# Score operands in two float32r parts, scores over the row groups of the array, merged mask and maximum, and bias rows in the matmul, in a one-core decoder layer

## The chip, the core and the metric

The kernel runs on one core of a Trainium2 chip. A core has a matrix engine (PE, with its weight loads listed apart as PEld), a vector engine (DVE), a scalar engine (ACT), GpSimd (POOL), and a queue engine (SP) that issues DMA transfers. On-chip memory is SBUF; matmuls write to PSUM, which has eight banks of 128 x 512 float32. Every engine runs its own instruction stream in order, and semaphores connect the streams. The metric is device time in microseconds from one launch; the profile's span reaches from the first to the last instruction.

## What is computed

One decoder layer over 32 batches of 128 tokens, width 512, in float32: self-attention of 16 heads with rotary embedding and a causal mask, cross-attention over the token axis (8 heads of 16 tokens, 512 x 512 scores for each head), and a feed-forward part with ternary weights and activations in int8 steps. A layer norm follows each.

```python
x = _layernorm(x + _L0_attn_ref(x, Wq, Wk, Wv, Wo))          # softmax(mask(q k^T / sqrt(32))) v
x = _layernorm(x + _L0_xattn_ref(x, ctx, ctx, gamma))        # q, k, v: [batch, 8 heads, 16, 512]
#   qk = einsum('bhdq,bhdl->bhql', qh, kh) / 4;  ret = einsum('bhql,bhdl->bhdq', softmax(qk), vh)
x = _layernorm(x + _L0_ffn_ref(x, w1, b1, ln_g, ln_b, w2, b2))
#   h = silu(bitlinear158(x, w1, b1)); h = gelu(h); h = layer_norm(h, ln_g, ln_b)
#   return bitlinear158(h, w2, b2)    # act_quant(rms_norm(x)) @ weight_quant(w).T + b
```

## The kernel before

**Two phases.** Phase one does the self-attention of all 32 batches and prepares the operands of the cross-attention in DRAM. Phase two does the cross-attention and the feed-forward part, again batch by batch. Work of several batches overlaps inside each phase.

**The order.** The class `Plan` fixes the order of every engine's instructions before the program runs. Each operation has a kind ("PE.sc"), a cost in microseconds, inputs, outputs and a priority; of the operations that could come next, the one is taken that can start first by these costs, with ties by priority plus an offset per kind (`OFF1`, `OFF2`). The order is then fixed with dependencies, so an engine waits for the next instruction in its list even if a later one could go. All transfers are issued from SP, in order. Transfers that prefetch have a release time: 17.8 us a batch in phase one and 30 us a batch in phase two.

**Phase one, per batch.** `project` (L322) multiplies with float32 accuracy in three one-pass float32r products of high and low parts, twelve matmuls of 128 x 512 for q, k, v and the output projection each. `rope` rotates, transposes (L402) turn q and k, and `head` (L412) does four heads at a time: h counts the 32-row groups of the transposed q and k, and c the four chunks. For each h there are four float32 matmuls into one bank (L419), the mask is added on DVE (L422), the maximum is taken (L425), ACT computes four exponentials with their sums (L430), and the weights are divided by the sums (L435) and transposed (L442). `stage_o` weighs the values (L461, four column groups in turn), projects and normalizes. `split3` (L326) writes q and the context as three bfloat16 parts, on DVE, POOL and ACT, and stores six copies of parts for each (L339). PSUM is divided by use: three banks for projections, three for transposes, one for scores, one for the weighed sums.

**Phase two, per batch.** For each group of four heads, `b1_` computes all scores once to find the largest of every query: 16 matmuls of 96 rows in bfloat16 (L653; six products of parts for each of 16 tokens), each followed by a maximum on DVE (L657). `shift` splits the negated maxima into three bfloat16 parts on POOL (L676 to L680), transposes them (L685), copies them on DVE (L687) and stores them as three further rows of the query operand (L691). `b2_` then computes the scores turned, with 99 rows (L746), takes exponentials on ACT (L749), and sums with the context (L756). `final` divides, adds and normalizes through small transfers: F (L767), den (L828), num (L829), rd (L835), rden (L836), and x1 (L830). `up_` quantizes the rows (`scales`, `steps`), multiplies with the ternary weights (L933) and lets DVE scale and add the bias b1 (L936) into z. `gelu_` (L942) is one ACT operation of silu and gelu over 2048 columns, so its table loads stand together. `down_` normalizes z (L963; parts of 512 columns, the first on ACT at L780, the others on POOL), scales it by g and b (L980), quantizes it in two halves on ACT (L897) and DVE (L899) with a conversion (L902), multiplies (L1017), and adds to x2 + b2, which POOL made (L920).

## Time and profile before

Three runs took 1843.21, 1843.22 and 1847.17 us. The profiled execution is one more.

| what | value |
|---|---|
| median of the runs | 1843.22 us |
| span of the profiled execution | 1837.6 us |
| mean granted PE clock | 0.960 of full speed |
| last score of phase one (L419) | 663.2 us |
| first score of phase two (L653) | 683.5 us |
| last maximum of phase two (L657) | 1713.1 us |
| DMA | 275.75 MB, mean 150 GB/s |

The profile's page splits the span into 40 slices and gives the busy share of each in tenths. PE's weight loads are at 7 of ten in the first 14 slices and at 2 to 3 after them, which shows the two phases. Its groups by line give, for each kind of instruction, busy time, the mean of one, and the idle time in front of it with the releaser. The durations of one engine can overlap, above all PE's, so two counts are used in this document: the duration of a group, and the distance between the starts of neighbours in the timeline.

### The profile page before, as it was taken

How to read it: one execution, taken by the hardware profiler on the slowest of the kernel's cores; microseconds unless marked ns; L12 is line 12 of the kernel's file. 1: busy time of each engine (PE TensorE's matmuls, PEld its weight loads, DVE VectorE, ACT ScalarE, POOL GpSimd, SP SyncE). 2: the span in 40 equal slices, each digit the busy share in tenths (PEclk: the TensorE clock that was granted, in tenths of full speed). 3: DMA queues.
4: the chain of work that ended last, by engine and by line, in shares of the span. 5: the costliest groups of instructions: out<-in, count | busy, mean ns of one | idle time of the engine just before them, and what ended most of it. 6: DMA issues, size and time to landing. Idle time of an engine off the chain costs nothing.

```text
span 1837.6 us, 29788 instructions
## 1 busy us (share of the span) xinstructions
PE 1694.8 (92%) x9540; PEld 848.8 (46%) x9540; DVE 1630.8 (89%) x2811; ACT 1337.6 (73%) x2811; POOL 1256.5 (68%) x1903
## 2 busy tenths in 40 slices
PE   6999999999999989999999999999999998889864
PEld 5877777777777762232323333333333322222221
DVE  7789998889988868898989999999999989999885
ACT  3556545664545544789999989999999979878862
POOL 4466666656656550467798989899889986775562
PEclk9999999999999987998999999999999999989976
DMA  6466656665654564543545455454544543533422
GB/s 197 136 212 210 193 191 205 210 212 187 203 175 161 174 212 171 149 116 106 148 122 159 110 134 147 126 149 117 151 137 128 154 118 110 147 106 102 97 61 57
DMA packets 237733, 275.75 MB, mean 150 GB/s; under 512 B 112124, under 2 KB 161276, under 8 KB 237192
## 3 DMA queue, kind: packets, MB, share of 16 engines
q1 hardware_dynamic: 237576, 273.85, 50.2%
q8 instruction: 75, 1.23, 0.3%
q14 instruction: 82, 0.67, 0.1%
HBM read 150.82 MB, written 101.20 MB: 137 GB/s over the span
## 4 chain that ended last, share of the span: by engine, by line
PE 47%; DVE 23%; DMA 9%; ACT 7%; POOL 6%; issue 4%; SPq 1%; DVEq 0%; POOLq 0%; ACTq 0%
PE mm L322 14%; DVE mt L657 7%; PE sT L746 7%; PE acc L756 7%; PE mx L653 6%; PE sc L419 5%; ACT ex L749 3%; PE m L933 3%; PE m L1017 2%; DMA qd<-sp 2%; PE tr L442 2%; DMA q2T<-q 1%; DVE z L936 1%; DVE pr L422 1%; DMA qp<-qd 1%
## 5 line engine op out<-in xcount | busy, mean ns | idle before, releaser
L657 DVE TENSOR_REDUCE mt<-mx 128x1 f32<-128x512 f32 x1024 | 642.4, 678 | 42.7 <-PE mx L653 41.5
L749 ACT ACTIVATE ex<-sT 128x512 f32<-128x512 f32 x1024 | 535.6, 618 | 90.7 <-PE sT L746 71.8
L653 PE MATMUL mx<-kp,qp 96*128 96x512 bf16 x1024 | 342.3, 393 | 34.4 <-DVE mt L657 28.4
L746 PE MATMUL sT<-qp,kp 99*128 99x512 bf16 x1024 | 322.9, 388 | 10.8 <-ACT ex L749 6.3
L756 PE MATMUL acc<-ex,cT 128*32 128x512 f32 x2048 | 275.7, 613 | 0.7 <-DMA cT<-cd 0.7
L430 ACT ACTIVATE pr<-pr,nm 128x128 f32<-128x128 f32 x512 | 199.5, 392 | 103.9 <-DVE nm L425 87.2
L653 PEld LDWEIGHTS <-qp 96*128 96x128 bf16 x1024 | 96.5, 99 | 221.9 <-issue 120.9
L746 PEld LDWEIGHTS <-kp 99*128 99x128 bf16 x1024 | 88.3, 98 | 222.5 <-issue 146.5
L445 ACT COPY prT<-tr 128x512 f32<-128x512 f32 x96 | 52.9, 587 | 149.2 <-PE tr L442 149.0
L419 PE MATMUL sc<-qkT,qkT 32*128 32x128 f32 x1024 | 147.8, 283 | 11.6 <-DVE pr L422 11.1
L933 PE MATMUL m<-w1q,q1T 128*128 128x512 fp8e4 x512 | 137.4, 392 | 22.0 <-DVE z L936 12.4
L419 PEld LDWEIGHTS sc<-qkT,qkT 32*128 32x128 f32 x1024 | 123.4, 186 | 52.2 <-DVE pr L422 22.1
L980 POOL TENSOR_TENSOR z<-z,g_b 128x512 f32<-128x512 f32 x108 | 139.5, 1302 | 4.9 <-ACT z L780 4.3
L980 POOL TENSOR_TENSOR z<-z,bb_b 128x512 f32<-128x512 f32 x108 | 139.8, 1301 | 1.4
L435 POOL TENSOR_TENSOR pr<-pr,rd 128x512 f32<-128x512 f32 x96 | 106.4, 1108 | 45.9 <-DVE rd L433 31.8
L386 POOL TENSOR_TENSOR ra<-ra,rb 128x256 f32<-128x256 f32 x64 | 47.3, 738 | 117.4 <-DVE rb L381 117.1
L1017 PE MATMUL m<-w2q,q2T 128*128 128x512 fp8e4 x432 | 112.3, 388 | 3.8 <-DMA q2T<-q 2.8
L422 DVE TENSOR_TENSOR pr<-sc,cmask 128x512 f32<-128x512 f32 x128 | 86.8, 678 | 18.3 <-PE sc L419 10.1
L1017 PEld LDWEIGHTS <-q2T 128*128 128x128 f16 x512 | 52.3, 104 | 105.0 <-DMA q2T<-q 29.1
L936 DVE SCALAR_TENSOR_TENSOR z<-m,dq,b_b 128x512 f32<-128x512 f32 x128 | 94.9, 741 | 6.0 <-PE m L933 5.4
L430 ACT ACTIVATION_READ_ACCUMULATOR pr<-pr,nm 128x1 f32 x512 | 96.5, 189 | 0.0
L756 PEld LDWEIGHTS acc<-ex,cT 128*32 128x32 f32 x2048 | 41.2, 108 | 119.5 <-issue 112.8
(159 smaller groups left out, 3475.3 us busy)
## 6 DMA issues: line engine op xcount, KB each, us to landing
kd<-sp SPq DMA_DIRECT2D x192, 128.0 KB
qd<-sp SPq DMA_DIRECT2D x192, 128.0 KB
kp<-kd SPq DMA_DIRECT2D x64, 384.0 KB
qp<-qd SPq DMA_DIRECT2D x64, 384.0 KB
cd<-v SPq DMA_DIRECT2D x32, 512.0 KB
cT<-cd SPq DMA_DIRECT2D x32, 512.0 KB
F<-f SPq DMA_DIRECT2D x64, 256.0 KB
xt<-in_xT SPq DMA_DIRECT2D x32, 256.0 KB
```

Of the source, the lines that this page charges most:

```text
L322: nc.tensor.matmul(pq.t, parts[a].t[:, c, :], w[t][:, c, sl], start=k == 0, stop=k == 11)
L419: nc.tensor.matmul(sc.t[:, c * P:(c + 1) * P], qT.t[r, c, :], kT.t[r, c, :], start=True, stop=True)
L430: nc.scalar.activation(pr.t[:, c, :], pr.t[:, c, :], AF.Exp, bias=nm.t[:, c:c + 1], accum_out=den.t[:, c:c + 1])
L653: nc.tensor.matmul(sc.t[:, j, :], q.t[0:NPR, h, (qc + j) * P:(qc + j + 1) * P], k.t[0:NPR, h, :], start=True, stop=True)
L657: pl.op("DVE.mx", 0.064 + 0.534 * W, lambda: nc.vector.tensor_reduce(mt.t[:, i:i + W], sc.t, AX.X, ALU.max), (sc,), (mt,), p, join=True)
L746: nc.tensor.matmul(sc.t[:, i, :], k.t[:, h, lc * P:(lc + 1) * P], q.t[:, h, :], start=True, stop=True)
L749: pl.op("ACT.ex", 0.052 + 0.426 * SW, lambda: nc.scalar.activation(ex.t[:, j:j + SW, :], sc.t, AF.Exp, scale=1.0 / XD ** 0.5), (sc,), (ex, ...
L756: nc.tensor.matmul(acc.t[32 * h:32 * h + 32, :], v.t[:, XH * lc + 4 * g + h, :], exs[h // 2].t[:, h % 2, :], start=lc == 0, stop=lc == NC - 1)
L933: nc.tensor.matmul(flat(pz)[:, i * 512:(i + 1) * 512], q1T.t[:, c, :], w1q[:, c, (n + i) * 512:(n + i + 1) * 512], start=c == 0, stop=c == ...
L936: pl.op("DVE.z", 0.13 + 0.535 * W, lambda: nc.vector.scalar_tensor_tensor(z.t[:, sl], flat(pz), dq1.t, b1_b[:, sl], ALU.mult, ALU.add), (p ...
L980: pl.op(e + kind, 0.148 + 0.0021 * w if e == "Pool" else 0.05 + 0.00105 * w, lambda: en(e).tensor_tensor(t(), t(), other[:, sl], op), src, ...
L1017: nc.tensor.matmul(flat(py)[:, 0:D], q2T.t[:, c, :], w2q[:, c, :], start=c == 0, stop=c == NI - 1)
```

## The change

**Phase one.** The scores of all four groups of heads become one operation of 16 matmuls, chunk by chunk over the four row groups, into four banks. Adding the mask and taking the maximum become one call for each chunk, of the negated masked score and its minimum; the exponential then has scale -1. The split makes two float32r parts instead of three bfloat16 ones, and two transfers of 256 KB each. All eight banks of PSUM are shared by all uses, in both phases. The biases b1 and b2 are split in two parts and stored as three rows each.

**Phase two.** A score operand has 48 rows (three products of parts for 16 tokens) and one row for the shift. Two heads lie in one tile, at partitions 0 and 64. The maxima are transposed in float32, without the split. An operand is fetched in four transfers instead of one. The bias enters as a last matmul of three rows, scaled by the inverse of the row's scale (`inverse`), so that silu on ACT reads PSUM directly with the row's scale. Silu is four operations of 512 columns, and a window in the planner keeps exponentials of other batches out between a batch's first silu and its gelu. The normalization of z is all on POOL, and the second quantization is one addition on POOL and one subtraction on DVE. The sums with the context are cut into two halves of 256 columns, but for the first chunk. The planner prices the second of two neighbouring score matmuls of opposite halves at 0.06 us, and a table load at 1.28. Offsets, buffers and release times (15 and 29 us a batch) are set anew, and comments are gone.

```diff
-NPR = 6 * XD
-NROW = NPR + 3
+NPR = 3 * XD
+NROW = NPR + 1
+HALF = 64
...
+            if o.engine == "PE":
+                if o.half is not None and self.half == 1 - o.half and t < self.free.get("PE", 0.0) + 0.02:
+                    o.end, self.half = t + self.BESIDE, None
+                else:
+                    self.half = o.half
+            if o.tab:
+                if self.table not in (None, o.tab):
+                    o.end += self.LOAD
+                self.table = o.tab
+                self.window = None if o.closes else o.win
...
+    def fetch(t, d, g, keys):
+        rows = t.bitcast(F32).rearrange("(p r) j c -> p r j c", p=2)
+        src = d[:, :, 4 * g:4 * g + 4, :].rearrange("s t (p j) c -> p (s t) j c", p=2)
+        for p in range(2):
+            if keys:
+                nc.sync.dma_start(rows[p, 0:XD], src[p, 0:XD])
+                nc.sync.dma_start(rows[p, XD:NPR], src[p])
+            else:
+                nc.sync.dma_start(rows[p, 0:2 * XD], src[p])
+                nc.sync.dma_start(rows[p, 2 * XD:NPR], src[p, 0:XD])
...
-                ("sp", C1["sp"], (P, 3, D), BF16), ("spr", C1["spr"], (P, D), F32), ("cx", 2, (P, D), F32),
+                ("sp", C1["sp"], (P, 2, D), F32R), ("cx", 2, (P, D), F32),
...
-            for s, k in enumerate(parts):
-                dma(kind, lambda s=s, k=k: nc.sync.dma_start(dst[s].rearrange("t h c -> h t c"), sp.t[:, k, :]), 131,
+            pl.op(f"{e1}.{kind}l", 0.6 if e1 == "DVE" else 1.225, lambda: en(e1).tensor_tensor(
+                sp.t[:, 1, :], v.t, sp.t[:, 0, :].bitcast(F32), ALU.subtract), (v, sp), (sp,), prio)
+            for s in range(2):
+                dma(kind, lambda s=s: nc.sync.dma_start(dst[s].rearrange("t h c -> h t c"), sp.t[:, s, :].bitcast(F32)), 262,
                     (sp,), (), prio)
...
+            scs = [pl.buf("sc") for _ in range(4)]
+            def scores():
+                for c in range(NC):
+                    for h in range(4):
+                        r = slice(32 * h, 32 * h + 32)
+                        nc.tensor.matmul(scs[h].t[:, c * P:(c + 1) * P], qT.t[r, c, :], kT.t[r, c, :],
+                                         start=True, stop=True)
+            pl.op("PE.sc", C1['scc'], scores, (qT, kT), scs, at + 0.2)
...
-                pl.op("DVE.mask", 0.6, lambda: nc.vector.tensor_tensor(
-                    pr.t, sc.t.rearrange("p (a b) -> p a b", b=S), cmask.unsqueeze(1).to_broadcast([P, 4, S]), ALU.add),
-                    (sc,), (pr,), p)
-                pl.op("DVE.nm", 0.6, lambda: nc.vector.tensor_reduce(nm.t, pr.t, AX.X, ALU.max, negate=True),
-                      (pr,), (nm,), p)
+                def top():
+                    for c in range(NC):
+                        nc.vector.tensor_tensor_reduce(pr.t[:, c, :], sc.t[:, c * P:(c + 1) * P], cmask, -1.0, 3e38,
+                                                       ALU.add, ALU.min, nm.t[:, c:c + 1])
+                pl.op("DVE.mask", 0.8, top, (sc,), (pr, nm), p)
...
+            def half(h):
+                sc, i, r = pl.buf("mx"), 8 * h + 4 * j + qc, slice(HALF * h, HALF * h + NPR)
+                pl.op("PE.mx", 0.23, lambda: nc.tensor.matmul(sc.t, q.t[r, j, qc * P:(qc + 1) * P], k.t[r, j, :],
+                                                             start=True, stop=True), (q, k), (sc,), p, half=h)
...
+            m = 1 if lc == 0 else 2
+            for i in range(m):
+                pl.op("PE.pv", 0.96 / m, lambda cols=slice(D // m * i, D // m * (i + 1)), last=lc == NC - 1 and i == m - 1: weigh(cols, last), exs + [v], (acc,), p)
...
+        def inverse():
+            e = en(e2)
+            r = ut.t.rearrange("p (g r) -> p g r", r=32)
+            if e2 == "DVE":
+                nc.vector.reciprocal(u.t, dq.t)
+            else:
+                nc.gpsimd.tensor_tensor(u.t, dq.t, none, ALU.pow)
+            e.tensor_scalar(r[:, :, 0:3:2].bitcast(F32R), u.t.unsqueeze(2).to_broadcast([P, 4, 2]), 1.0, None, ALU.mult)
+            e.tensor_tensor(r[:, :, 1], u.t.to_broadcast([P, 4]), r[:, :, 0], ALU.subtract)
...
-            pl.op("DVE.z", 0.13 + 0.535 * W, lambda: nc.vector.scalar_tensor_tensor(z.t[:, sl], flat(pz), dq1.t, b1_b[:, sl],
-                                                                         ALU.mult, ALU.add), (pz, dq1, consts[0]), (z,), at, join=True)
+                if last:
+                    nc.tensor.matmul(pz.t, uT.t[32 * n:32 * n + 3, :], rows1[32 * n:32 * n + 3, :], start=False, stop=True)
+            pl.op("ACT.silu", 0.478, lambda: nc.scalar.activation(z.t[:, sl], pz.t, AF.Silu, scale=dq1.t),
+                  (pz, dq1), (z,), at, join=True, tab="silu", win=win)
...
+                if n == 7:
+                    nc.tensor.matmul(py.t, uT.t[0:3, :], rows2, start=False, stop=True)
```

In the settings, `q2m='ad'` becomes `q2m='mp'`, `zm='APPP'` becomes `zm='PPPP'`, and the buffers `x2` 2 to 4, `z` 3 to 4 and `q1T` 2 to 4. In the changed file the scores of phase one are L469, the merged mask L481, the two scores of phase two L716 and L779, the sums L788, and silu L983.

## The prediction

> **What bounds the kernel now.** The change touches both phases, so I first split the span with the view of busy time by stretch and then price each phase in its steady part.

> ```profile
> span 1837.6 us, 29788 instructions
> PE 1694.8 (92%) x9540; PEld 848.8 (46%) x9540; DVE 1630.8 (89%) x2811; ACT 1337.6 (73%) x2811; POOL 1256.5 (68%) x1903
> ...
> 350.00:400.00 50.00, 49.44 (x325) 39.79 (x324) 39.81 (x78) 31.21 (x111) 30.91 (x38) 1.00 0.69 232
> ...
> 950.00:1250.00 300.00, 287.23 (x1488) 93.18 (x1485) 284.52 (x467) 279.61 (x417) 267.88 (x451) 0.99 0.49 133
> ```

> Columns: stretch, its length, busy time of PE, PE's weight loads, DVE, ACT, POOL, granted clock, DMA share, GB/s. Phase one is one engine's: PE never stops (49 of 50 us); DVE averages 88% from 100 to 600 us. Phase two has four loaded engines: DVE 95%, ACT 93%, POOL 89%, and a PE figure that overlapping records inflate. The DMA queues are half empty and the clock is full: neither bounds.

> Periods: the stores of x1 stand at 96.1 and 420.9 us with 16 batches between, so **20.3 us a batch** in phase one. The silu table loads stand at 918.5 and 1182.0 with 8 between: **32.9 us a batch** in phase two. Per batch of phase two that makes DVE 31.2 us, ACT 30.7, POOL 29.4 (284.52, 279.61, 267.88 over 9.1 batches).

> PE has to be counted start to start, from its timeline:

> ```profile
> 333.53 1.10 PE L322 MATMUL mm<-woh,ol 128*128 128x512 f32 x4
> 334.47 0.60 PE L402 MATMUL tr<-ident,ra 128*128 128x128 f32 x4
> 334.82 1.18 PE L322 MATMUL mm<-wol,oh 128*128 128x512 f32 x4
> ...
> 337.77 1.15 PE L419 MATMUL sc<-qkT,qkT 32*128 32x128 f32 x8
> 338.85 1.08 PE L461 MATMUL po<-prT,v 128*32 128x128 f32 x32
> 339.86 1.20 PE L322 MATMUL mm<-wvh,xh 128*128 128x512 f32 x4
> 340.99 1.15 PE L419 MATMUL sc<-qkT,qkT 32*128 32x128 f32 x8
> 342.08 1.20 PE L322 MATMUL mm<-wvh,xl 128*128 128x512 f32 x4
> ...
> 1107.65 0.81 PE L746 MATMUL sT<-qp,kp 99*128 99x512 bf16 x3
> 1108.39 1.06 PE L756 MATMUL acc<-ex,cT 128*32 128x512 f32 x8
> 1109.39 0.82 PE L746 MATMUL sT<-qp,kp 99*128 99x512 bf16 x3
> 1110.05 0.38 PE L653 MATMUL mx<-kp,qp 96*128 96x512 bf16 x1
> ```

> Read the starts, not the lengths. Four projection matmuls take 0.94 us undisturbed (333.53 to 334.47), 0.233 each. One head's scores (four fp32 matmuls, eight records) take 1.08. Sixteen matmuls into four column groups in turn (L461) take 1.01: four run beside each other. Three 512-wide bf16 scores take 0.66, 0.217 each, and 0.74 where the tiling of the array changes behind them: **about 0.1 us a switch** (likewise 1.13 against 0.94 before L419). PE per batch, phase one: 48 x 0.233 = 11.2, scores 4 x 1.08 = 4.3, 24 transposes about 2.4, L461 1.0, ten switches 1.0: 19.9 of the 20.3. Phase two: 64 scores x 0.217 = 13.9, eight sums of about 0.86 = 6.9, feed-forward 32 x 0.216 = 6.9, transposes 0.35, 16 switches 1.6: 29.7 of 32.9. So phase one is PE's; phase two is DVE's by a little.

> **Phase one.** *Scores in turn.* The 16 matmuls of four heads become one operation whose neighbours use different row groups. L461 is the nearest row: 1.01 us for as many, so four times faster than 4.3. [...] Ends 1.0 and 3.5; I take 1.4, near the row. Six switches go too: 0.6 us. PE becomes 11.2 + 1.4 + 2.4 + 1.0 + 0.4 = 16.4.

> *Mask and maximum merged.* A head had two DVE passes 0.60 us apart, 4.8 us a batch. After, the compiled stream has 512 instructions of 128x128 and 512 that read an accumulator. A 512-wide pass of 0.60 is 0.53 of stream and 0.07 fixed, so 128 wide is 0.20 (0.28 if the full 0.145 of its duration, 678 - 533 ns, shows); a 128x1 read lies between 0.06 (start to start) and 0.19 (ScalarE's read, L430). 16 x 0.28 = 4.5 us, between 4.2 and 7.5: **no real gain**. The two-part split is where DVE gains: casts of 0.64 and 0.55 and one of two subtractions of 0.97 go, 2.2 us. DVE: 17.9 - 0.3 - 2.2 = 15.4 (15.1 to 18.4), below PE. POOL loses one subtraction (1.3), ACT nothing. SP issues 4 split writes a batch instead of 12, at 0.65 each. The scores now take four of eight shared banks at once, held until DVE has read them, 1.1 us a head; projections keep the other four. Before, such waits cost PE 11 us in all; after I add 0.8 us a batch (0 to 1.5). Period 17.2, so 3.1 x 31 = **-96 us** (-108 to -43).

> *The seam.* At the end of phase one the chain of waits is the split writes of the last batches, two of four such pieces:

> ```profile
> 682.81 5.41 DMA qd<-sp
> 688.24 5.41 DMA qd<-sp
> ```

> Six issues per 5.4 us become two with two thirds of the bytes: 1.8 (by bytes) to 3.5 us (by issues) less, four times: -10 us.

> **Phase two.** *Pairs of row halves.* The bf16 scores of 96 rows become float32r of 48 or 49 rows at partition 0 or 64. In the changed program's order the 2048 score matmuls fall into 1248 slots if neighbours of opposite halves share one: 39 a batch. Float32r costs 0.233 (L322): 39 x 0.233 = 9.1 us for 13.9. No row here shows halves beside each other, only column groups (L461), which share fully. So 9.1, bounded by 64 x 0.233 = 14.9.

> *Weights.*

> ```profile
> L653 PEld LDWEIGHTS <-qp 96*128 96x128 bf16 x1024 | 96.5, 99 | 221.9 <-issue 120.9 <-DVE mt L657 11.3 <-DMA qp<-qd 2.1
> L322 PEld LDWEIGHTS mm<-wqkl,xh 128*128 128x128 f32 x256 | 48.5, 192 | 12.3
> ```

> The columns end in count, busy time, mean ns: a load takes 99 ns in bf16, 192 in float32r. With loads starting 0.11 us apart (L419) two fit beside one matmul, sum 9.1; by the full 0.19 a pair lasts 0.38 and 25 pairs add 3.7 us. I take the start spacing, since L322 hides its loads.

> *Switches* are what speaks most against the change. The order has 51 a batch instead of 16, because half-height score tiles lie between full-height feed-forward matmuls, bias rows have three rows only, and six of eight sums are cut in two 256-wide halves. [...] By the row a switch is 0.1: 35 x 0.1 = 3.5 us. [...] I take the row. Bias rows add five matmuls, 1.1 us, the fp32 transposes 0.25. PE: 9.1 + 6.9 + 6.9 + 1.1 + 0.6 + 5.1 = **29.7, as before**.

> *DVE*: four z passes go at 0.66 (-2.65). The second quantisation swaps 1.06 + 0.86 for one 2048-wide pass, nearest row 1.33 (L899): -0.6. The inverse scales add twice reciprocal, scale, difference and copy, 0.16 + 0.25 + 0.2 + 0.21: +1.65. 29.6. *ACT*: -0.84 (zt), -1.18 (q2), silu in four from PSUM +0.17: 28.9. *POOL*: x2b -1.34, shift parts -2.53, nb -0.19, a fourth zt +0.8, 2048-wide q2 +2.6 (four of 0.73, less fixed parts): 28.7. All four engines end at 28.7 to 29.7. The period was 1.055 of the largest sum (32.9 / 31.2): 31.3.

> *A new wait.* From a batch's first silu to its gelu no exponential may run. Silu waits for PE's four groups of about 1.3 us; behind it on ACT stand the exponentials, behind those the score banks and PE's sums. At worst 4 x 1.3 - 4 x 0.52 = 3.1 us a batch, at best nothing (squares and copies fill it). I add 0.7: period 32.0, 0.9 x 31 = **-28 us** (-59 to +20). SP issues 12 more operand loads a batch at 0.43 and two fewer shift stores: about 4 us more on some 16 of 33. The sum chain F, den, rd, rden queues behind them, but has slack of whole batches: nothing; up to 1 us a batch without it.

> **Sum**: 1837.6 - 96 - 10 - 28 = 1703.6 in the span; the median lies 5.6 us above the span: **1709 us** (one case: 1670 to 1750).

> **Rivals.** *Weights load one after another* (for it: 0.11 spacing in L419; against: column groups show none): scores 3.5, period 18.9, -43; the rest as above: **1762**. *Halves and groups do not share the array*: scores stay 4.3 and phase one keeps only the switches (-19); phase two's PE is 35.5, period 36.2, +3.3 x 31 = +102: 1911, **1916 us, slower**. It decides once the second of a pair costs over 0.17 us while phase one gains only 43. For it: no pair in this trace; against: L461. *The order fits badly*: it is fixed in advance, and the planner's costs hold no price for a switch; engines of equal load then wait on each other, period 34: +34 for -28, **1771**. *Everything hides*: switches free, no silu wait, -108 and -59: **1666**. That the change does not do what it says holds for the merged mask: 1024 instructions for 256; alone it takes DVE to 18.4, period about 18.7: 1755, inside the range.

> **Numbers.** Forecast 0.50, serial weights 0.20, bad order 0.06, all hidden 0.10, slower 0.14. No change to be told (within 0.3%, about what a measurement of this kernel resolves) gets 0.03 out of the bad order: faster 0.83, same 0.03, slower 0.14. Range 1655 to 1840: it takes in all but the slower rival and the lowest tail.

> **What would show it.** Sixteen L469 scores in 1.4 us right, 3.5 wrong. Stores of x1 17.2 us apart. Neighbouring L716 halves starting within 0.05 us; if 0.2, the slower rival. Table loads 32 us apart, DVE near 93%, ACT idle before silu under 1 us a batch. Wrong overall if phase two's period grows past 34.

## The result and the profile after

The changed kernel took 2006.21 us in the median of four runs (1975.96 to 2026.27), against 1843.3 of before on the same chip: a ratio of 1.079, interval 1.071 to 1.087. Ratios leave out executions over 1.5% above a kernel's fastest, so they can lie under the ratio of the medians beside them. The forecast was 1709. Phase one did what was predicted: from the first matmul of PE (TensorE in the recorded texts) to the first score of phase two it takes 574.8 us in place of 675.0. Phase two, from its first score to the last matmul, takes 1411.2 us in place of 1147.3. So 100 us were won and **264 us lost**. These, from the page of the changed kernel, are the span, the busy times and the granted clock in 40 slices:

```profile
span 2002.6 us, 34163 instructions
PE 1870.9 (93%) x11300; PEld 915.7 (46%) x11300; DVE 1491.7 (74%) x3547; ACT 1325.9 (66%) x2853; POOL 1174.5 (59%) x1599
...
PEclk8999999999985877998778767788978776696986
```

The clock row of before, from its page:

```profile
PEclk9999999999999987998999999999999999989976
```

In phase one (the first 11 slices of after) both rows read 9, but for the first slice of after. In phase two the row of before reads 9 nearly throughout, and the row of after 6 to 9: the mean granted clock fell from 0.960 to 0.851. The busy times of two stretches of after (stretch, length, then PE, weight loads, DVE, ACT, POOL, clock, DMA share, GB/s), one in each phase:

```profile
300.00:400.00 100.00, 96.21 (x798) 76.56 (x799) 82.40 (x321) 64.15 (x237) 70.64 (x86) 1.00 0.69 221
1100.00:1200.00 100.00, 99.76 (x461) 36.51 (x461) 63.68 (x112) 65.22 (x104) 58.44 (x80) 0.71 0.38 99
```

and the second stretch in before:

```profile
1100.00:1200.00 100.00, 96.71 (x511) 31.34 (x511) 96.84 (x160) 94.98 (x146) 89.94 (x155) 1.00 0.52 141
```

DVE, ACT and POOL, which were 90 to 97% busy, now stand at 58 to 65%, while PE has hardly a gap. The groups of after say whom the other two wait for (count, then busy time and mean ns, then idle time before them and its releasers):

```profile
L718 DVE TENSOR_REDUCE mt<-bank 128x1 f32<-128x512 f32 x1024 | 654.3, 682 | 272.5 <-PE bank L716 258.4 <-PE bank L779 10.7
L781 ACT ACTIVATE ex<-bank 128x512 f32<-128x512 f32 x1024 | 542.6, 606 | 263.8 <-PE bank L779 226.0 <-PE bank L716 24.2 <-PE bank L788 6.5
```

Both wait for scores. The timeline of PE in after shows how these run, first where the granted clock is a half, then where it is full:

```profile
1102.56 0.79 PE L779 MATMUL bank<-qp,kp 49*128 49x512 f32 x1
1103.15 0.63 PE L716 MATMUL bank<-kp,qp 48*128 48x512 f32 x1
1103.15 0.79 PE L779 MATMUL bank<-qp,kp 49*128 49x512 f32 x1
1103.75 0.62 PE L716 MATMUL bank<-kp,qp 48*128 48x512 f32 x1
1103.75 1.05 PE L779 MATMUL bank<-qp,kp 49*128 49x512 f32 x2
...
1416.05 0.61 PE L1060 MATMUL bank<-w2q,q2T 128*128 128x512 fp8e4 x2
1416.58 0.49 PE L716 MATMUL bank<-kp,qp 48*128 48x512 f32 x1
1417.01 0.60 PE L1060 MATMUL bank<-w2q,q2T 128*128 128x512 fp8e4 x2
...
1419.96 0.50 PE L779 MATMUL bank<-qp,kp 49*128 49x512 f32 x2
1420.30 0.40 PE L716 MATMUL bank<-kp,qp 48*128 48x512 f32 x2
1420.63 0.60 PE L1060 MATMUL bank<-w2q,q2T 128*128 128x512 fp8e4 x2
```

The reader sees three things. Halves do share the array here: two scores start at 1103.15, and four scores fit between 1419.96 and 1420.63. A score that stands alone between feed-forward matmuls takes 0.43 us (1416.58 to 1417.01), twice the 0.215 us at which 512-column scores of before follow one another; what the changes of the array's tiling around it have in this is taken up with the pairs below. And at half clock a pair takes 0.60 us.

**Where the 264 us are.** I counted PE's phase two from start to start, separately for full and half clock, taking out stretches of over 1.3 us without a start. A score takes 0.250 us in the mean at full clock in after (before: 0.260), and 0.37 at half. Pricing every matmul at half clock at its excess over the same kind at full clock gives 212 us in after and 43 in before: **the clock is 169 of the 264**. At full clock after's 64 scores take 16.0 us a batch (before 16.6), the sums 8.4 (8.1), the feed-forward 8.1 (7.4), and the bias rows and their transposes, which before has not, 2.7. The changes of these four (-0.6 + 0.3 + 0.7 + 2.7 = 3.1 us a batch, 99 us) make the rest, some 95 us; idle time is about the same.

**What the clock goes by here.** The records of the clock in these traces change in steps of 3.41 us. For each such window I added the columns that the matmuls stream in it, each weighted by its rows/128 and its weight columns/128, and divided by the columns that a window can stream at full clock (512 in 0.215 us). A record of a float32 matmul that is neither float32r nor a transpose counts twice: one of the sums takes 0.125 us with four column groups side by side (L756 of before, eight in 1.00 us), so 0.50 us for its 512 columns. Time in use does not tell windows apart: PE is over 92% busy in every 100 us of after from 600 to 1700 us. This share of the array's cells does:

```
kernel               windows that end     windows that stay     windows at
                     the full clock       at full clock         half clock
                     (median, largest)    (10th pct., median)   (after 150 us)
before               0.27, 0.38           0.54, 0.75             41
after                0.28, 0.37           0.45, 0.61            172
tall halves          0.29, 0.36           0.49, 0.62             90
before, short scores 0.27, 0.36           0.48, 0.60            166
full filler          0.27, 0.36           0.46, 0.56            127
score twice          0.29, 0.36           0.45, 0.58            154
```

In these windows the bound lies near 0.37, and a window at half clock behind which the full clock came back has about as much (0.34 to 0.37 at least); a few windows kept it with less, down to 0.28. Over the 3241 windows of the six kernels, the best single bound on the cells (0.36) puts 42 on the wrong side of whether the next window is full or half. With rows alone it is 340, with weight columns alone 289, with the columns streamed 465, with time in use 606. So the clock of after comes down even where PE does not stop: of the 28 windows at full clock behind which after fell to half, 13 touch no idle gap of over 0.5 us, while in before 18 of 20 touch one of over 1 us.

That is the trap: at half clock even the feed-forward's matmuls of 128 x 128 x 512 follow one another at 0.427 us in place of 0.215 (before, medians), which is a share of 0.5, and a pair of 48 rows each in 0.60 us uses 2 x 0.215 x 0.375 / 0.60 = 0.27. (Only pairs in the middle of a run come 0.43 us apart there, for 0.38.) So scores tend to hold the half clock that a short stall or they themselves brought. The experiments test this theory ("cells") against the rivals: too much work or too many switches, slow loads of the four-byte operands, a bad order.

### The profile page after: what moved, and what is told of

Its sections match the earlier page's. It is cut to its first block, busy times and chain, and to the rows that moved or that the text cites. A ratio compares the mean times of both kernels' runs of the same rounds, so it can differ in the third digit from the quotient of the medians.

```text
span 2002.6 us, 34163 instructions
## 1 busy us (share of the span) xinstructions
PE 1870.9 (93%) x11300; PEld 915.7 (46%) x11300; DVE 1491.7 (74%) x3547; ACT 1325.9 (66%) x2853; POOL 1174.5 (59%) x1599
## 5 line engine op out<-in xcount | busy, mean ns | idle before, releaser
L718 DVE TENSOR_REDUCE mt<-bank 128x1 f32<-128x512 f32 x1024 | 654.3, 682 | 272.5 <-PE bank L716 258.4
L781 ACT ACTIVATE ex<-bank 128x512 f32<-128x512 f32 x1024 | 542.6, 606 | 263.8 <-PE bank L779 226.0
L716 PE MATMUL bank<-kp,qp 48*128 48x512 f32 x1024 | 381.5, 530 | 15.5 <-DVE ya L527 6.8
L779 PE MATMUL bank<-qp,kp 49*128 49x512 f32 x1024 | 377.1, 563 | 11.2 <-DMA qp<-mT 3.5
L788 PE MATMUL bank<-ex,cT 128*32 128x256 f32 (+1 forms) x3584 | 360.2, 497 | 0.0
L779 PEld LDWEIGHTS bank<-qp,kp 49*128 49x128 f32 x1024 | 155.2, 218 | 248.5 <-ACT ex L781 102.0
L716 PEld LDWEIGHTS bank<-kp,qp 48*128 48x128 f32 x1024 | 172.5, 224 | 168.6 <-DVE mt L718 62.7
L1060 PE MATMUL bank<-w2q,q2T 128*128 128x512 fp8e4 x512 | 177.6, 455 | 14.1 <-DMA q2T<-q 12.4
L978 PE MATMUL bank<-w1q,q1T 128*128 128x512 fp8e4 x512 | 162.2, 434 | 1.3 <-DMA q1T<-q 1.1
L983 ACT ACTIVATE z<-bank,dq 128x512 f32<-128x512 f32 x128 | 86.0, 686 | 101.3 <-PE bank L980 100.9
L788 PEld LDWEIGHTS bank<-ex,cT 128*32 128x32 f32 x3584 | 85.5, 118 | 146.4 <-issue 120.5
L481 DVE CUSTOM_DVE_ANT_0 pr<-banka,cmask 128x128 f32<-128x128 f32 x512 | 110.8, 284 | 24.8 <-PE banka L469 24.8
```

What stands on the lines that cost most here:

```text
L481: nc.vector.tensor_tensor_reduce(pr.t[:, c, :], sc.t[:, c * P:(c + 1) * P], cmask, -1.0, 3e38, ALU.add, ALU.min, nm.t[:, c:c + 1])
L716: pl.op("PE.mx", 0.23, lambda: nc.tensor.matmul(sc.t, q.t[r, j, qc * P:(qc + 1) * P], k.t[r, j, :], start=True, stop=True), (q, k), (sc,), ...
L718: pl.op("DVE.mx", 0.598, lambda: nc.vector.tensor_reduce(mt.t[:, i:i + 1], sc.t, AX.X, ALU.max), (sc,), (mt,), p, join=True)
L779: pl.op("PE.sT", 0.23, lambda: nc.tensor.matmul(sc.t, k.t[r, j, lc * P:(lc + 1) * P], q.t[r, j, :], start=True, stop=True), (k, q), (sc,), ...
L781: pl.op("ACT.ex", 0.478, lambda: nc.scalar.activation(ex.t[:, h, :], sc.t, AF.Exp, scale=1.0 / XD ** 0.5), (sc,), (ex,), p, join=True, tab ...
L788: nc.tensor.matmul(acc.t[32 * h:32 * h + 32, cols], v.t[:, XH * lc + 4 * g + h, :], exs[h % 2].t[:, h // 2, cols], start=lc == 0, stop=last)
```

## The experiments

**One part alone: phase one.** The phase one of after ahead of the phase two of before.

```diff
-                pl.op("PE.sc", 0.875, scores, (qT, kT), (sc,), p)
+            scs = [pl.buf("sc") for _ in range(4)]
+            pl.op("PE.sc", C1['scc'], scores, (qT, kT), scs, at + 0.2)
...
-            pl.tag(name, n, ps, (P, D))
+            pl.tag(name, C1[name], group="bank")
```

> The phase one of the change (sixteen scores in turn over the four row groups, merged mask, shared banks) ahead of the phase two of the kernel before, with the three-part operands left as they were. Theory (the loss is all in phase two, where the granted clock falls because the half-height scores fill too few of the array's cells): 1740 us, between 1725 and 1765, granted clock about 0.96, that is the 1843 of before less the 105 us by which the last score of phase one comes earlier in the changed kernel. Rival (phase one leaves the chip in a state that brings the clock down later): over 1850, clock under 0.9.

Measured 1814.34 us, ratio 0.985 (0.981 to 0.988), clock 0.95. The theory's side is right, its size not: the first score of phase two came at 648.5 us after the first matmul, not at 575. Part of that was mine: the loads kept the release of 17.8 us a batch. The second try:

> The new phase one ahead of the phase two of before, once more, now with the offsets and the pace of 15 us a batch of the changed kernel in the plan of phase one (the first such kernel kept loads released at 17.8 us a batch, and offsets of before where the changed kernel had none). Theory: phase one ends as in the kernel with old operands, 614 us to the first score of phase two in place of 648, and phase two takes its 1148 us: 1778 us, between 1762 and 1796. Rival (the three-part operands themselves hold phase one back): 1814 within 10.

Measured **1778.61 us, ratio 0.965 (0.963 to 0.967)**: the first score of phase two at 606.9, phase two 1156. Phase one is sound, and this kernel beats both. Two kernels below that have the two-part split as well get there at 592 and 594; what makes the rest of the way to the 574.8 of after is open.

**One part undone: the score operands.**

```diff
-NPR = 3 * XD
+NPR = 6 * XD
...
-nc.tensor.matmul(sc.t, q.t[r, j, qc * P:(qc + 1) * P], k.t[r, j, :], start=True, stop=True)
+nc.tensor.matmul(sc.t, q.t[0:NPR, h, qc * P:(qc + 1) * P], k.t[0:NPR, h, :], start=True, stop=True)
```

> The changed kernel with one part undone: the scores of phase two take the three-part bfloat16 operands of 96 and 99 rows again, one score at a time; the bias rows, the sigmoid from the banks, the shared banks and the new phase one stay. Theory (share of the cells): clock back to about 0.96 and 1700 us, between 1670 and 1760. Rival A (too many switches or too much work in the pairs) gives the same here and is told apart by the two kernels with extra matmuls. Rival B (the bias rows, the silu read from the banks or the order of the plan is what stops phase two): stays above 1900.

Measured 1951.62 us, ratio 1.058 (1.053 to 1.063), clock 0.935. The clock came back most of the way, the time did not: rival B, whose mark was over 1900, has a part in it. Phase two took 1332 us, 185 more than before, with PE at 38.1 us a batch and 3.6 idle. By the count from start to start the bias rows and their transposes are 2.4 us a batch, 75 of the 185, and idle time some 48; the plan had to be drawn anew, so its order has changed too.

**More work for the array.** Two kernels with 512 extra matmuls in the same places.

```diff
+if h == 0:
+    nc.tensor.matmul(sc.t, idle[0:128, :], w1q[0:128, 0, 0:D], start=True, stop=True)
 nc.tensor.matmul(sc.t, q.t[r, j, qc * P:(qc + 1) * P], k.t[r, j, :], start=True, stop=True)
...
+for _ in range(2 - h):
     nc.tensor.matmul(sc.t, q.t[r, j, qc * P:(qc + 1) * P], k.t[r, j, :], start=True, stop=True)
```

> The changed kernel with more work: ahead of every first score of a pair in the maxima, one matmul of 128 rows by 128 columns by 512 whose result the score then overwrites, 16 a batch, 512 in all. Theory (share of the cells): each fills the whole array for 512 columns, the window shares stay above the bound, the clock goes to 0.95 or more, and the time falls in spite of the work: 1800 us, between 1720 and 1880. Rivals (TensorE has too much to do, too many switches, or the order is bad; or the clock goes by busy time alone, which is 98% already): the work is added to a TensorE that never idles, 512 times 0.23 to 0.60 us: 2120 to 2310 us.

> The control of the kernel with the full-height filler: in the same places the same number of extra matmuls of 512 columns, but each is the first score of the pair once more, so it covers 48 of 128 rows. TensorE is kept just as busy as by the filler. Theory (share of the cells): the shares stay near or under the bound, the clock stays at about 0.8 in phase two, and the time grows to about 2200, between 2050 and 2320. Rival (busy time decides, or a fuller queue by itself): the same time as the full-height filler, within 30 us.

Measured 2124.18 and 2069.14 us (ratios 1.135 and 1.119). The first time is missed by far and lies where the rivals had put it; the second is at the low end of its range. The clock did what the theory says: over four runs each 0.895 to 0.928 with the full filler, 0.856 to 0.878 with the score twice, 0.843 to 0.872 in after, though PE is over 94% busy in every 100 us of the full filler from 600 to 1700 us, as it is over 92% in after. But the full filler has its price, which I had left out. Its group:

```profile
L721 PE MATMUL bank<-w1q,idle 128*128 128x512 fp8e4 x512 | 221.7, 433 | 10.4 <-DVE ya L529 7.1
```

Each one stands between row tiles, so it breaks a run of scores. From start to start it took 0.32 us at full clock, and the scores beside it rose from 0.25 to 0.27. The fillers' own time (512 x 0.32 = 164 us) and the dearer scores (some 45) outweigh the 60 us or so by which the excess of half clock fell. So these two kernels speak for the theory by their clock alone, and a test without new switches was needed.

**The same instructions, more rows.** The shift moves to row 63 of each half and rows 48 to 62 hold zeros; the order of every engine is that of after, instruction for instruction, but for eight memsets ahead of phase two that write the zeros.

```diff
-NROW = NPR + 1
+NROW = HALF
+SHIFT = HALF - 1
...
-r = slice(HALF * h, HALF * h + NPR)
+r = slice(HALF * h, HALF * h + SHIFT)
```

> The changed kernel with the same instructions in the same order on every engine, but each half-height score contracts 63 (maxima) or 64 rows (weights) in place of 48 and 49: the shift stands in the last row of the half and the rows between hold zeros, so the sums are the same. Nothing else of TensorE's work, its switches or its pairs is touched. Theory (the clock goes by the share of the array's cells in use): the share of a score rises by 1.31, fewer windows fall under the bound, the clock rises from 0.85 to 0.90 or more, and the time falls to 1920 us, between 1860 and 1965. Rivals (switches, work, busy time, order; or rows of zeros don't count): 2006 us within 25, clock 0.85.

Measured **1871.33 us, ratio 1.013 (1.008 to 1.018)**, clock 0.918 to 0.944: 135 us less than after by the medians, 122 by the ratios, for rows that add nothing to the result. Of its four executions the profiled one is the longest. Against the profiled one of after its span is 111 us less (1891.7 for 2002.6), and by the count above its excess of half clock is 111 us less too (101 for 212). Its clock row:

```profile
PEclk9999999999998898998979787998988899889876
```

Neither the matmuls, the switches, the loads nor the order changed, so none of those rivals explains this part. That rows of zeros count (0.918 to 0.944 for the 0.843 to 0.872 of after) shows that here it is the rows addressed, not what is in them.

**The mirror: fewer rows in before.** Only its slices change.

```diff
-q.t[0:NPR, h, (qc + j) * P:(qc + j + 1) * P], k.t[0:NPR, h, :]
+q.t[0:48, h, (qc + j) * P:(qc + j + 1) * P], k.t[0:48, h, :]
...
-k.t[:, h, lc * P:(lc + 1) * P], q.t[:, h, :]
+k.t[0:48, h, lc * P:(lc + 1) * P], q.t[0:48, h, :]
```

> The kernel before, in its own order, with the scores of phase two contracting the first 48 of their 96 and 99 rows: three of the six products of parts, and no shift, so the weights keep the leading part of the keys only. Columns streamed, instructions and operands loaded are the same. Theory (cells): the share of a score is halved, the granted clock falls from 0.96 to under 0.90 and the time grows to 1960 us, between 1900 and 2100, though there is less to compute. Rival (rows don't matter to the clock; only the switches to a 64-row tile cost, 15 to 30 a batch at 0.1 us): 1843 to 1930 with the clock at 0.95 or more.

Measured 2028.98 us, ratio 1.097 (1.088 to 1.105), clock 0.846 to 0.870: less to multiply, and 185 us more. Clock and score group of its page:

```profile
PEclk8999999999899755775789959999999986786776
...
L653 PE MATMUL mx<-kp,qp 48*128 48x512 bf16 x1024 | 389.1, 446 | 22.2 <-DVE mt L657 15.9 <-DVE mT L687 1.8 <-DMA qp<-qd 1.2
```

At full clock a score takes 0.270 us from start to start, as with 96 rows (0.271); 286 of the 1024 run at half clock in place of 60. By the count above the excess of half clock is some 220 us in place of 43, nearly all of the loss. The switches to the scores of 48 rows show in the feed-forward matmuls ahead of them (0.248 us for 0.229 in the mean, 20 us in all), and less idle time makes up for them.

**Are the pairs worth it?** Full height without pairs, and pairs always issued together.

```diff
-k = qk.tile([P, 2, D], F32R, tag=f"kp{i}", name=f"kp{i}")
+k = qk.tile([P, 2, 2, D], F32R, tag=f"kp{i}", name=f"kp{i}")
...
-r = slice(HALF * h, HALF * h + NPR)
+r = slice(0, 2 * NPR)
...
-nc.tensor.matmul(sc.t, q.t[r, j, qc * P:(qc + 1) * P], k.t[r, j, :],
+nc.tensor.matmul(sc.t, q.t[r, j, qc * P:(qc + 1) * P], k.t[r, h, j, :],
```

> The changed kernel with its two-part operands, but no pairs: the rows of two heads lie under one another (96, and two of shift), the keys are kept twice with zeros under the other head, and every score is one matmul of 96 or 98 rows, so it uses three quarters of the rows and no row tile is switched to. Two of eight buffers of the weights are given up for the room. Theory (cells): clock 0.93 or more in phase two, TensorE at full clock as in the changed kernel (a score took 0.25 us there in the mean, since the pairs were lost in short runs), so 1850 us, between 1780 and 1920. Rival (pairs do save their half of the time and the clock is no matter): 64 scores of 0.23 us a batch in place of 39 slots add 6 us a batch: 2100 us or more.

Measured 2001.87 us, ratio 1.088, clock 0.924 to 0.938. The clock is about right, the time wrong: scores cost 0.317 and 0.301 us from start to start, not 0.25. (Some 0.03 of that is booked to the score in place of the feed-forward matmul ahead of it, whose record is that much shorter here: 0.21 us for 0.25.) The weight loads differ:

```profile
L718 PEld LDWEIGHTS bank<-kp,qp 96*128 96x128 f32 x1024 | 196.7, 200 | 200.9 <-DVE mt L720 105.6 <-issue 40.0 <-ACT ex L783 10.5
```

Such a four-byte load takes 200 ns here, a bfloat16 one of before 99. In the middle of a run of scores it hardly shows: full-height scores follow at 0.235 us in place of 0.215. Next to the sums it does: from the last sum ahead to the first behind, one score takes 0.74 us here and 0.63 in the kernel with the old operands. What a run of scores between two feed-forward matmuls takes at full clock, from the start of the last one ahead to the start of the first one behind (medians in us, 0.216 of them the feed-forward's own):

```
scores in the run                           1      2      3      4
before (96, 99 rows, bfloat16)            0.435  0.650
before, short scores (48 rows, bfloat16)  0.630  0.846  1.062
full height, no pairs (96, 98, float32r)  0.449  0.694  0.922  1.158
after (halves of 48, 49, float32r)        0.739  0.743  0.978  0.982
```

A pair inside a run costs 0.24 us, as one score of full height does. But to go from full height to the halves and back costs 0.29 us in after, where the short bfloat16 scores pay 0.20, two switches of 0.1. So a run of one pair (0.743) is dearer there than two bfloat16 scores of full height (0.650). Between sums, whose column groups change the tiling anyway, one and two scores take 0.74 us in after, 0.74 and 0.97 at full height and 0.63 and 0.85 with the old operands: the halves cost nothing more, and a pair saves 0.11. After has 20.3 runs a batch, of 3.2 scores in the mean. Scores and feed-forward together come to 23.8 us a batch in after, 23.7 in before and 26.2 at full height without pairs: what pairing saves, the wider operand had cost.

```diff
+scs = [pl.buf("mx") for _ in range(2)]
...
+pl.op("PE.mx", 0.3, scores, (q, k), scs, p)
...
-half(h)
+top(h)
```

> The changed kernel with the two scores of a pair issued as one step of the plan, so that they always follow one another (four buffers each for maxima and weights in place of three): 16.6 runs of scores a batch in place of 20.3, none of odd length. Theory (a run of scores costs its slots of 0.22 us and about 0.2 us more for draining in and out of the row tiles; the clock goes by cells): 39 slots become 32 and 3.7 runs fall away, 2.3 us a batch at full clock and more at the mean clock, and the clock rises a little: 1910 us, between 1850 and 1960. Rival (sharing the array is worth nothing here, only the clock counts): 2006 us within 30.

Measured 2037.41 us, ratio 1.106 (1.101 to 1.111), clock 0.85. A miss: at full clock scores are a little cheaper (0.257 and 0.217), but PE stands idle for 132 us in place of 63. A pair needs two free banks at once: of the idle time ahead of its first scores and their loads, DVE's maxima, which give banks back, end the most (129 us). The 0.2 us a run of the expectation is two switches at 0.1; that the array drains at one is not shown by a run.

**What is left in the tall kernel.** Three kernels on its base; the first two lines of the diff go in the kernel without bias rows and in the one with the rows unissued, the others in the one with whole sums.

```diff
-nc.tensor.matmul(pz.t, uT.t[32 * n:32 * n + 3, :], rows1[32 * n:32 * n + 3, :], start=False, stop=True)
-nc.tensor.matmul(py.t, uT.t[0:3, :], rows2, start=False, stop=True)
...
-m = 1 if lc == 0 else 2
+m = 1
```

> The kernel with tall halves, without the biases of the feed-forward: the three-row matmuls that add them, the transposes that make their rows and the steps on VectorE before them are left out, so b1 and b2 are missing from the result. Theory (they are TensorE's work on the path: five matmuls of 0.43 us and two transposes of 0.22 us a batch, and their switches): 2.7 to 3.5 us a batch less: 1775 us, between 1745 and 1800. Rival (covered by other waits): 1871 within 20.

> The kernel with tall halves, with the weighted sums no longer split in two halves of 256 columns: the runs of scores fall from 20.3 to 15.9 a batch and the switches from 43.7 to 33.4. Theory (a switch costs 0.1 to 0.2 us of a TensorE that bounds phase two): 1 to 2 us a batch less: 1825 us, between 1795 and 1850. Rival (the split is worth its switches, since scores come sooner): 1871 or more.

> The kernel with tall halves in its own order, instruction for instruction, but for the five three-row matmuls a batch that add the biases of the feed-forward, which are not issued (b1 and b2 are missing from the result; their transposes and the steps before them stay). The first try at this left them out of the plan too, which drew a different order and came out slower. Theory (they stand on the path of a TensorE that bounds phase two, at 0.43 us each, and use 3 of 128 rows for the clock): 70 to 110 us less: 1780 us, between 1755 and 1810, clock up by 0.01 or more. Rival (hidden in other waits): 1871 within 20.

With the biases left out of the plan, 1920.07 us (1.041); with whole sums, 2068.03 (1.120): both do less or switch less, and both are slower. Each draws a new order from offsets that were found for another set of operations, and PE idles 119 and 146 us where the tall kernel idles 70. With the order kept and only the five matmuls not issued, the ratio is 0.993 (0.990 to 0.997) against 1.013: 0.020 of 1843, **about 36 us**, half of the least that I expected (25 us by the medians, 1846.27 of ten executions for 1871.33). So for the bias rows the new order cost more than leaving them out gave, and a comparison is fair only where the order stands still; for the whole sums no run with the order held was made.

**New phase one, operands in two parts, feed-forward and order of before.** Tall pairs, and full height unpaired.

```diff
-pl.op("ACT.silu", 0.478, lambda: nc.scalar.activation(z.t[:, sl], pz.t, AF.Silu, scale=dq1.t),
+pl.op("DVE.z", 0.13 + 0.535 * W, lambda: nc.vector.scalar_tensor_tensor(z.t[:, sl], flat(pz), dq1.t, b1_b[:, sl],
```

> The new phase one with two-part operands, then a phase two made of the paired scores in their tall form (63 and 64 rows, zeros between) and, for all the rest, the feed-forward, the banks, the order and the settings of the kernel before: bias by VectorE and GpSimd, sums unsplit, no bias rows, no transposes for them. Theory (what is left of the loss in the tall kernel is the bias rows and the shorter runs of scores, 20.3 a batch against 14.8 here; half-height scores that are tall enough keep the clock): 575 us of phase one and at most the 1148 us of the phase two of before: 1723 us, between 1695 and 1760, clock 0.94 or more. Rival (half-height scores pull the clock down whatever stands beside them): over 1800, clock under 0.92.

> The new phase one with two-part operands, then the phase two of before with its order and settings, its scores read from two-part operands at full height (96 and 98 rows: two heads under one another, the keys kept twice with zeros under the other head), unpaired. Theory: 575 us of phase one and the 1148 us of before, and a weight load of 0.20 us in place of 0.10 that shows 0.05 us a score, 3 us a batch at most: 1755 us, between 1715 and 1800, clock 0.94 or more. Rival (the loads are never hidden): over 1820.

Measured 1817.54 us (0.986) and 1819.00 (0.988). They miss by 95 and 64 us: phase one ends at 592 and 594 us, and phase two takes 1209 and 1201, above the 1147 of before. At full height the scores took 0.300 and 0.291 us in place of 0.271 and 0.248, which is 2.3 us a batch, but 1.2 of it is taken off the feed-forward matmuls ahead of them, as above; the 1.0 that is left is 33 of the 54 us lost, and longer idle time the rest. In the tall one 75 windows ran at half clock in place of 41, 71 us of excess in place of 43, at a clock of 0.924 to 0.929, between the theory's mark and the rival's. Neither beats the kernel with the new phase one alone.

**The parts of phase one**, on that kernel.

```diff
-for c in range(NC):
-    for h in range(4):
+for h in range(4):
+    for c in range(NC):
```

> The kernel with the new phase one at its own pace and the phase two of before, with the two loops of the sixteen scores exchanged: four scores of one row group follow one another, then the next group. Theory (only neighbours in different row groups share the array; the 0.875 us for four of before comes back): 2.2 to 2.9 us a batch more on TensorE, phase one is bound by it: 1855 us, between 1825 and 1880. Rival (sharing gives nothing, the gain of phase one is in the banks and the mask): 1779 within 6.

Measured 1818.81 us, 40 more, a little under the range. The timelines of PE, first this kernel, then after:

```profile
354.27 2.82 PE L463 MATMUL banka<-qkT,qkT 32*128 32x128 f32 x32
357.01 1.20 PE L366 MATMUL banka<-wqkh,xh 128*128 128x512 f32 x4
```

```profile
329.30 1.17 PE L469 MATMUL banka<-qkT,qkT 32*128 32x128 f32 x32 [0.90 <-DVE qkT L455]
330.40 1.20 PE L377 MATMUL banka<-wqkh,xh 128*128 128x512 f32 x4
```

The same 16 scores take 2.74 us from start to start in one order and 1.10 in the other. So neighbours in different row groups share the array; 1.64 us over 32 batches is 52, of which 40 show.

```diff
-for c in range(NC):
-    nc.vector.tensor_tensor_reduce(pr.t[:, c, :], sc.t[:, c * P:(c + 1) * P], cmask, -1.0, 3e38,
-                                   ALU.add, ALU.min, nm.t[:, c:c + 1])
+nc.vector.tensor_tensor(pr.t, sc.t.rearrange("p (a b) -> p a b", b=S),
+                        cmask.unsqueeze(1).to_broadcast([P, 4, S]), ALU.add)
+nc.vector.tensor_reduce(nm.t, pr.t, AX.X, ALU.max, negate=True)
```

> The kernel with the new phase one at its own pace and the phase two of before, with mask and maximum taken apart again as in the kernel before (one addition and one reduction of 512 columns for a head). Theory (merging is no gain: four steps of 0.28 us with four reads of 0.08 us a head against two of about 0.6 us): 1779 us within 8. Rival (the merging is what VectorE gains in phase one): 1795 or more.

Measured 1826.95 us: 48 more, so the rival was right. The DVE groups between 100 and 500 us, first apart (76 heads, 19 batches), then merged (84 heads, 21 batches):

```profile
L476 DVE TENSOR_REDUCE nm<-pr 128x4 f32<-128x512 f32 x76 | 52.2, 686 | 2.7
L474 DVE TENSOR_TENSOR pr<-banka,cmask 128x512 f32<-128x512 f32 x76 | 51.7, 680 | 2.7 <-PE banka L463 2.1 <-PE banka L493 0.6
```

```profile
L475 DVE CUSTOM_DVE_ANT_0 pr<-banka,cmask 128x128 f32<-128x128 f32 x336 | 73.6, 282 | 2.4 <-PE banka L463 1.6 <-PE banka L493 0.7
...
L475 DVE DVE_READ_ACCUMULATOR2_ANT nm<- 128x1 f32 x336 | 26.9, 80 | 0.0
```

Busy time, not count times mean, is what counts: neighbours overlap by 0.06 us, so merged costs 100.5 / 21 = 4.8 us a batch and apart 103.9 / 19 = 5.5. That is 0.7 us, 22 us in all, of a DVE that is 91% busy here. What makes it 48 was not tried.

## Why the prediction was wrong

**The step that failed** is the sentence "The DMA queues are half empty and the clock is full: neither bounds." It was true of before and was carried over to after without asking what holds the clock up. Every PE term of phase two was then priced at full clock. The change takes half of the rows from the scores, and the clock's excess grew from 43 to 212 us: 169 of the 264 lost. The two kernels that change rows alone show it from both sides: 111 us of excess and 111 us of span less with tall halves, some 180 us of excess and 185 us more with short scores. Long idle gaps do not account for after: of its 28 windows at full clock behind which the clock fell to half, 5 touch an idle gap of over 3.4 us, about the length of a window.

**The second term** that failed is PE's sum at full clock, "29.7, as before". Counted from start to start it rose by 3.1 us a batch. Scores fell by 0.6, where -4.8 for pairs and +3.5 for switches had been set, -1.3 together; bias rows and their transposes took 2.7 in place of 1.35; feed-forward and sums rose by 1.0, set at nothing beyond their switches. The slots were counted well, and a pair inside a run does take the 0.233 of the forecast (0.24). But runs are short: one between feed-forward matmuls pays 0.29 us to get to the halves and back, where two switches at 0.1 are right for bfloat16 alone (0.20), and one between sums pays 0.11 for float32r. The prediction weighed the load (3.7 us if it shows in full) and took nothing.

**Right in mechanism.** The sixteen scores took 1.10 us (forecast 1.4; no run shows that term, and the runs show 1.10 in turn and 2.74 group by group), and the 3.5 at the other end, 32 loads at the 0.11 us of L419 (eight loads in 0.96 us in before, one 0.19 long), did not come true either: the 32 loads of L469 take 0.98 us in after. The scores came 17.0 us apart (30.4 to 557.1 us in 31 steps; forecast 17.2), the second of two neighbouring halves starts 3 ns behind the first, and phase one with its seam gave 100 us (106). The forecast "no real gain" of the merged mask was wrong: the merged form came out near its price (4.8 us a batch for 4.5; the 0.53 of stream and 0.145 fixed in it are those of before, where a reduction of 2048 columns takes 2271 ns, L1006, and one of 512 takes 678, L657), but the two passes apart take 5.5 in busy time, not the 4.8 that it set against them, and undoing the merge costs 48 us. So that phase one came so near its sum is in part luck.

**The rivals.** The one on the slow side, 1916 us because halves do not share the array, named the wrong mechanism: they share. "The order fits badly" was given 6 in 100 and 34 us. It has a part: the kernel with old operands had its clock at 0.935, and its phase two still took 185 us more than that of before, though 75 of these are bias rows and their transposes. The test set beforehand, a period beyond 34 us, was met: 1411 us over 32 batches is 44.

**Open.** Of the 264 us, the rows settle 111 to 135 and the bias matmuls about 36. The rest lies in the half clock that the tall kernel still has (101 us of excess in its longest run, 43 in before), in the way to the halves and back, and in an order whose worth could not be taken apart from its operations. The bound near 0.37 is read from windows, not set by a test of its own. That columns of weights count as rows do rests on the windows too (42 on the wrong side with both, 340 with rows alone), for no kernel changed them. Why going to the halves costs more in float32r than in bfloat16, the load or something else, was not set apart.

## What to carry to other kernels

Before cutting the rows of a matmul, add up what share of the array's cells the surrounding few microseconds use; where it comes near the 0.37 of these traces, a cheaper matmul can cost the clock, and unused rows filled with zeros can win part of it back with the same instructions (here 1871 us for 2006). Price pairs of row tiles by the length of the runs they stand in (here 0.24 us for each pair and 0.29 for each run between full-height matmuls), not by slots alone. Where a planner draws the order, test a part with the order held fixed: the kernels here that left work out under a new order came out 49 and 197 us slower.
